# Turning the normed tiles of a fused two-layer attention kernel: on TensorE, or through memory and VectorE

## The chip, the core and the metric

The kernel runs on one core of a Trainium2 chip. A core has five engines that run their own instruction streams in order and wait for one another through semaphores: TensorE (PE; its weight loads are listed apart as PEld), VectorE (DVE), ScalarE (ACT), GpSimd (POOL) and SyncE (SP). DMAs are issued from the queues of SP, ScalarE and GpSimd and run on 16 DMA engines. A matmul writes to PSUM, from where VectorE or ScalarE fetch the result; tiles lie in SBUF, 128 partitions wide.

The metric is the time of one execution on the device in microseconds, as the median of several runs.

## What is computed

Two layers over an image batch `x` of 8 x 32 x 32 positions with 512 channels, all in float32. The first is a self-attention over the 1024 positions of an image (group norm, query, key and value products, softmax over 8 heads of 64, output product, residual). The second is a deformable attention:

```python
x_ln = layernorm(x, ln_g, ln_b)
q = x_flat @ wq + bq
o = gelu(depthwise_conv_7x7_stride_2(q_img, dw_w) + dw_b)     # 16 x 16 positions
offsets = conv_1x1(o, pw_w)                                   # 2 channels
grid = reference points + tanh(offsets)
interp = grid_sample(x, grid)                                 # 256 sampled rows
k = v = interp @ wv + bv
qh, kh, vh = heads(q @ mq_w + mq_b), heads(k @ mk_w + mk_b), heads(v @ mv_w + mv_b)
att = softmax(qh @ kh.T) @ vh
z = att @ mo_w + mo_b + x
out = gelu(layernorm(z, ln_g, ln_b) @ mlp_w + mlp_b) + z
```

The last three lines are where the change lies: `z` is normalised row by row (positions on partitions), and the product with `mlp_w` needs it with channels on partitions, so each normed tile of 128 positions x 512 channels has to be turned.

## The kernel before

**Two passes.** The first pass (L407 to L840) runs layer 0 for the eight images in 256 units and writes its output (`mid`) and the layer norm of it (`hat_d`) to memory; the depthwise convolution of the first six images is done beside it. The second pass (L843 to L1298) runs layer 1. Its unit is one pair of heads of one half image: 512 queries against 256 sampled keys. Eight units make an image (half images of four units each), 64 units make the pass.

**Order.** Every instruction keeps the order of the program on its engine (`InOrder`, L43). The program's order is written out by hand: `at(place, step)` puts a step at a place counted in units, and `run_due` emits the steps sorted by place. So a place says only what stands in front of what, on each of the five queues, not when it runs. A step at 7.012 stands behind all of those at 7.0 and ahead of those at 7.02, on every queue on which it has instructions.

**A unit n** (`unit_steps`, L1188). At n the scores (32 weight loads, `sc<-keys,q`), VectorE's row maxima (`nmax`) and ScalarE's exponentials (`e`). At n + 0.02 and n + 0.04 `moved` turns e in blocks of 32x32 on VectorE (`sq<-e`) and sends it to memory (`sq_d`, SP); at n + 0.0401 `taken` brings it back with keys on partitions (`et`, SP), in all a transpose through memory; `share` and `spread` do the same with the reciprocal sums (`rs_d`, `inv`, SP). At n + 0.042 stands the next unit's query product (`mm<-hat_h,wqq`). At n + 1.1 the product with the values (`av<-et,vals`), at n + 1.2 VectorE scales it (`attH`). So `av` of a unit runs at the end of the next one.

**The tiles of a half image** (`back_steps`, L1107). When four units have filled `attH`, the next four units each take one tile t of 128 positions, at n = start + t: `fetch` and `add` bring x's row (`xr`, SP) and add the bias to it (GpSimd); `joined` at n + 0.012 is the output product (`mm<-wo,attH`) and VectorE's z, its statistics, and the reciprocal root on GpSimd (`mv`); `norm` at n + 0.03 makes `zn` (VectorE). `turned` at n + 0.6 has four transposes on TensorE (`mm<-ident,zn`), whose result ScalarE copies to `zT`; `mlp` at n + 1.03 is the product with `wm`, in front of the next query product; `biased` (VectorE), `gelu` (ScalarE, for two tiles at n + 1.72 of the odd one), `end` (GpSimd, n + 2.24) finish it. Where the pass ends (`over`, `eve`, `tail`), other places hold.

**Beside the units.** The convolution of images 6 and 7 runs in two lanes (`conv_steps`, L1217): lane 0 has its taps on VectorE (5 per unit, 3 in the units in which the points are at work), lane 1 has 7 per unit, multiplied on ScalarE (`parts`) and added on GpSimd (`chunk`). The points of the next image (`point_steps`, L1242) come from convolution and offsets: some 20 tiny operations on VectorE (`targets`), an indirect DMA of four rows (`gather`, GpSimd) and the weighted sum (`sample`, VectorE) for each half of the points. Before the units, `prep` (L904) multiplies weights together and `load_late` (L1258) loads the rest, among it `wm`.

Of the kernel before, what the change touches and what calls it, by code (L numbers as in the profile page):

```python
# [247 lines left out]
def attention_then_deformable_attention(  # L248
# [119 lines left out]
    def at(place, step):  # L368
        due.append((place, len(due), step))
# [473 lines left out]
    with ExitStack() as l1:  # L843
# [23 lines left out]
        def load_small():  # L867
            with nc.allow_non_contiguous_dma(reason="small vectors onto partitions"):
                for t, v in (
                    (bvk, mk_b), (bv_c, bv), (bvv, mv_b), (bqq, mq_b), (bq_c, bq), (lng, ln_g),  # L870
                    (lnb, ln_b),
                ):
                    nc.sync.dma_start(t, v.rearrange("(c p) -> p c", p=P))

        def load_conv():
            with nc.allow_non_contiguous_dma(reason="small vectors onto partitions"):
# [68 lines left out]

        def conv_fetch(b, cb):
            chat[b, cb] = cvhat.tile([P, NT, P], F32, tag="hat", name="hat", bufs=2)
            nc.sync.dma_start(chat[b, cb], hat_d[b][:, :, ts(cb, P)])

        def conv_load(b):  # L950
            room[b, "o"] = cv.tile([P, NC, NS], F32, tag="o", name="o")
            nc.sync.dma_start(room[b, "o"], o_d[b][:, :, :])

        def fill(b, cb, par):
            hat = chat[b, cb]
# [117 lines left out]

        def fetch_hat(hi):
            hat[hi] = raw.tile([P, NC, C], F32, tag="hat", name="hat_h", bufs=2)
            nc.sync.dma_start(hat[hi], hat_d[hi // 2][:, ts(hi % 2, NC), :])

# [24 lines left out]
        def tmp(name, bufs):  # L1104
            return work.tile([P, C], F32, tag=name, name=name, bufs=bufs)

        def back_steps(hi, start, step, tail=False):  # L1107

            b, half = divmod(hi, 2)
            xs = mid[b].rearrange("(t p e) c -> e t p c", e=2, p=P)[half]  # L1110
            outs = out_tok[b].rearrange("(t p e) c -> e t p c", e=2, p=P)[half]
            xr, z, zn, zT, res = {}, {}, {}, {}, {}
            n_units = 2 * B * NHP

            def fetch(t):
                xr[t] = tmp("xr", 4)
                nc.sync.dma_start(xr[t], xs[t])

            def add(t):
                nc.gpsimd.tensor_tensor(xr[t], xr[t], bo_row, ALU.add)  # L1120

            def joined(t):
                ps = project(lambda c: attH[hi][:, c, ts(t, P)], lambda c: wo[:, c, :])
                z[t] = tmp("z", 4)
                nc.vector.tensor_tensor(z[t], ps, xr[t], ALU.add)
                stats = work.tile([P, 6], F32, tag="stats", name="stats")
                mv = xr["mv", t] = work.tile([P, 3], F32, tag="mv", name="mv")
                nc.vector.bn_stats(stats, z[t])
                nc.vector.bn_aggr(mv[:, 0:2], stats)
                rstd(mv[:, 2:3], mv[:, 1:2], 1e-5)  # L1130

            def norm(t):
                zn[t], mv = tmp("zn", 2), xr["mv", t]
                nc.vector.tensor_scalar(
                    zn[t], z[t], mv[:, 0:1], mv[:, 2:3], ALU.subtract, ALU.mult
                )

            def turned(t):
                ps = mm_tile()
                for c in range(NC):  # L1140
                    nc.tensor.transpose(ps[:, ts(c, P)], zn[t][:, ts(c, P)], ident)
                zT[t] = tmp("zT", 2)
                for half in range(2):
                    nc.scalar.copy(zT[t][:, ts(half, C // 2)], ps[:, ts(half, C // 2)])

            def mlp(t):
                res["ps", t] = project(lambda c: zT[t][:, ts(c, P)], lambda c: wm[:, c, :])

            def biased(t):
                res[t] = tmp("res", 3)  # L1150
                nc.vector.tensor_tensor(res[t], res["ps", t], bm_row, ALU.add)

            def gelu(t):
                nc.scalar.activation(res[t], res[t], AF.Gelu)

            def end(t):
                (nc.vector if tail else nc.gpsimd).tensor_tensor(res[t], res[t], z[t], ALU.add)
                (nc.sync if tail else nc.gpsimd).dma_start(outs[t], res[t])

            for t in range(NC):  # L1160
                over, eve = (start + step * t >= n_units - i and not tail for i in range(2))
                n, pair = start + step * t, start + step * (t - t % 2)

                ends = (n + 0.6, n + 1.03, n + 1.0392)
                if eve:
                    ends = (n + 0.61, n + 0.72, n + 0.73) if over else (n + 1.06, n + 1.62, n + 1.625)
                places = (pair - 1.6, pair - 0.5), (n + 0.012, n + 0.03), ends
                if tail:
                    turn = n + 0.15 + 0.005 * (t > 0)
                    places = (n - 0.7, n - 0.6), (n, n + 0.01), (turn, n + 0.25, n + 0.26)  # L1170
                steps = (fetch, add), (joined, norm), (turned, mlp, biased)
                for place, what in zip(sum(places, ()), sum(steps, ())):
                    at(place, lambda t=t, what=what: what(t))


                ends = [t - 1, t] if t % 2 and not tail else [t] if tail else []

                for what, after in (
                    (gelu, 0.27 if tail else 0.735 if over else 1.72),
                    (end, 0.28 if tail else 0.74 if over else 2.24),  # L1180
                ):
                    for i in ends:
                        at(n + after, lambda i=i, what=what: what(i))
# [33 lines left out]
        def conv_steps():  # L1217
            for lane, chunks in enumerate(((0, 3, 6), (1, 2, 4, 5, 7))):
                free = 0.5 + lane
                for k in chunks:  # L1220
                    b, cb = EARLY + k // NC, k % NC
                    first = next(n for n in range(60) if n + 0.49 > free)
                    fills = [first + 0.49, first + 0.55]
                    at(fills[0] - 1.8, lambda b=b, cb=cb: conv_fetch(b, cb))
                    for par, place in enumerate(fills):
                        at(place, lambda b=b, cb=cb, par=par: fill(b, cb, par))
                        at(place + 0.02, lambda lane=lane, par=par: fill_end(lane, par))
                    unit = int(fills[1]) + 1
                    i = 0
                    while i < KS * KS:  # L1230
                        points = unit % (2 * NHP) in (NHP - 1, NHP, NHP + 2)
                        count = 7 if lane else 3 if points else 5
                        for j in range(count):
                            if i == KS * KS:
                                break
                            place = 0.25 + 0.01 * j if not lane else 0.045 + 0.001 * j if j < 4 else 0.65 + 0.01 * j
                            at(unit + place, lambda b=b, cb=cb, i=i, lane=lane: tap(b, cb, i, lane))
                            free = unit + place
                            i += 1
                        unit += 1  # L1240

        def point_steps(b):  # L1242
            last = 2 * NHP * b - NHP
            at(last - 3.5, lambda: conv_load(b))
            at(last - 2.035, lambda: conv_gelu(b))
            at(last - 1.465, lambda: offsets(b))
            at(last - 1.36, lambda: offsets_turned(b))
            at(last - 0.959, lambda: targets(b))
            for h, (p0, p1) in enumerate(((-0.28, 0.0415), (1.72, 2.0415))):
                at(last + p0, lambda h=h: gather(b, h))  # L1250
                at(last + p1, lambda h=h: sample(b, h))
            first = 2 * NHP * b
            for hp, place in enumerate((-0.82, -0.815, 0.185, 1.18)):
                at(first + place, lambda hp=hp: key_step(b, hp))
            for t, place in enumerate((-0.81, 0.18)):
                at(first + place, lambda t=t: value_step(b, t))

        def load_late():  # L1258
            nonlocal bq_row, wo, wm, bo_row, bm_row
            bq_row = load_row(wp, bq, "bq_row")  # L1260
            wo = load_w(late2, mo_w, "wo")
            wm = load_w(late2, mlp_w, "wm")
            bo_row = load_row(late, mo_b, "bo_row")
            bm_row = load_row(late2, mlp_b, "bm_row")
            load_conv()
# [66 lines left out]
```

## Time and profile before

Three runs took 3374.16 to 3378.19 us, with a median of 3374.57. The profiled execution:

| what | value |
|---|---|
| time of the profiled execution | 3374.83 us |
| its span, from the first to the last instruction | 3373.1 us |
| mean granted TensorE clock | 0.991 |
| first scores of the second pass, about | 2217.7 us |
| zn transposes, `mm<-ident,zn` | 256, busy 41.8 us |
| copies of them, `zT<-mm`, ScalarE | 128, mean 373 ns |
| block transposes, `sq<-e`, 128x1024, VectorE | 640, mean 1228 ns |
| block transposes, `rsT<-rs`, 128x32, VectorE | 128, mean 212 ns |
| `nmax<-sc`, VectorE | 640, mean 1214 ns |
| lane 0 taps, `chunk<-pad,dww,chunk`, VectorE | 144, mean 760 ns |
| lane 1 adds, `chunk<-parts,chunk`, GpSimd | 240, mean 787 ns |
| `xr<-mid`, SP, 256 KB | 64, landing after 6.0 us (median) |

How to read it: the busy time of TensorE is the union of matmuls that overlap one another, so a busy TensorE is not one at its peak. A group's mean mixes places with different neighbours. In a timeline each row is a run of like instructions: start, time, engine, operation, output<-inputs, count, and in brackets how long the engine was idle before it and what ended that. A DMA's "us to landing" runs from its issue to the semaphore that tells that its data is there.

### The profile page before, as it was taken

The page shows a single profiled execution, that of the slowest core. Times are in us where ns is not written, and L with a number is a line of the kernel's source. Part 1 is how long each engine was busy: PE and PEld are TensorE (multiplying, and loading weights), DVE is VectorE, ACT ScalarE, POOL GpSimd, SP SyncE. Part 2 cuts the span into 40 slices and gives each one's busy share as a digit, 9 for nine tenths or more (in the row PEclk, how much of TensorE's full clock was granted, in tenths as well). Part 3 has the DMA queues.
Part 4 walks back from the last instruction along what each step waited for, and adds up shares of the span by engine and source line. Part 5 has one row for each costly group of instructions (what it writes and reads, how often), then busy time and mean ns, then how long its engine had stood idle before and what let it go on. Part 6 is the DMA issues. An engine that isn't in the chain of part 4 may idle for free. (4 is left out here: it accounts for less than half of the span.)

```text
span 3373.1 us, 59630 instructions
## 1 busy us (share of the span) xinstructions
PE 3282.7 (97%) x21736; PEld 1339.8 (40%) x21736; DVE 2490.4 (74%) x3373; ACT 1809.0 (54%) x3927; POOL 1548.1 (46%) x1903
## 2 busy tenths in 40 slices
PE   7999999999999999999999998889999999999998
PEld 3344444444444344344344443433333333333333
DVE  5777788888888898888888886238667686665654
ACT  3443355576566566567567562135556555654442
POOL 1001226646746755764765663305555454642222
PEclk9999999999999999999999999999999999999999
DMA  5666766776766776766777766546666665665653
GB/s 150 179 179 164 209 181 186 223 182 183 214 188 181 210 201 181 210 197 183 204 196 184 203 193 180 170 139 220 192 206 198 191 200 187 214 218 191 224 181 127
DMA packets 446645, 642.56 MB, mean 190 GB/s; under 512 B 77105, under 2 KB 240945, under 8 KB 444305
## 3 DMA queue, kind: packets, MB, share of 16 engines
q1 hardware_dynamic: 415712, 536.67, 55.0%
q0 software_dynamic: 29488, 100.00, 9.7%
q8 instruction: 172, 2.82, 0.4%
q10 hardware_dynamic: 1152, 2.10, 0.2%
q14 instruction: 121, 0.98, 0.1%
HBM read 246.38 MB, written 123.73 MB: 110 GB/s over the span
## 5 line engine op out<-in xcount | busy, mean ns | idle before, releaser
L54 ACT ACTIVATE e<-sc,nmax 128x1024 f32<-128x1024 f32 (+1 forms) x1024 | 802.0, 796 | 494.5 <-DVE nmax L54 493.1
L54 DVE TENSOR_REDUCE nmax<-sc 128x1 f32<-128x1024 f32 (+1 forms) x640 | 751.3, 1214 | 337.5 <-PE sc L54 336.8
L54 POOL TENSOR_TENSOR oa<-part_x,oa 128x256 f32<-128x256 f32 x852 | 639.6, 751 | 554.0 <-ACT part_x L54 507.6
L54 DVE STREAM_TRANSPOSE sq<-e 128x1024 f32<-128x1024 f32 x640 | 766.1, 1228 | 155.8 <-ACT e L54 134.6
L54 ACT ACTIVATE part_x<-pad_x,dww_x 128x256 f32<-128x256 f32 x852 | 440.9, 545 | 250.3 <-POOL oa L54 249.4
L54 PE MATMUL sc<-k,q 64*64 64x512 f32 x4096 | 516.6, 602 | 13.5 <-ACT e L54 10.3
L54 PE MATMUL av<-et,v 128*64 128x256 f32 x4096 | 502.1, 388 | 15.1 <-DMA et<-sq 14.2
L54 PE MATMUL mm<-xT,wqkv 128*64 128x512 f32 x2048 | 463.5, 595 | 3.2 <-issue 3.2
L54 PEld LDWEIGHTS av<-et,v 128*64 128x64 f32 x4096 | 275.5, 137 | 332.6 <-issue 169.8
L54 POOL TENSOR_TENSOR chunk<-parts,chunk 128x256 f32<-128x256 f32 x240 | 188.8, 787 | 268.5 <-ACT parts L54 254.5
L54 POOL TENSOR_TENSOR mv<-mv,minus_half 128x1 f32<-128x1 f32 x128 | 76.3, 596 | 510.4 <-DVE mv L54 509.8
L54 PEld LDWEIGHTS sc<-k,q 64*64 64x64 f32 x4096 | 139.3, 132 | 321.8 <-issue 205.0
L54 PEld LDWEIGHTS mm<-xT,wqkv 128*64 128x64 f32 x2048 | 148.6, 138 | 255.0 <-issue 239.6
L54 DVE SCALAR_TENSOR_TENSOR od<-pad_x,dww_x,od 128x256 f32<-128x256 f32 x276 | 232.0, 841 | 5.5
L54 PE MATMUL mm<-wo,attH 128*64 128x512 f32 x1024 | 233.7, 598 | 0.0
L54 PE MATMUL mm<-wqkv,xT 128*64 128x256 f32 x2048 | 232.1, 379 | 0.0
L54 PE MATMUL mm<-wm,zT 128*64 128x512 f32 x1024 | 230.7, 592 | 1.0 <-ACT zT L54 1.0
L54 PE MATMUL mm<-w,attT 128*64 128x512 f32 x1024 | 229.8, 592 | 1.8 <-DVE attT L54 1.8
L54 PE MATMUL mm<-hat_h,wqq 128*64 128x512 f32 x1024 | 230.8, 593 | 0.0
L54 ACT ACTIVATION_READ_ACCUMULATOR e<-sc,nmax 128x1 f32 x1024 | 209.3, 204 | 0.0
L54 ACT ACTIVATE parts<-pad,dww 128x256 f32<-128x256 f32 x240 | 126.4, 551 | 126.8 <-POOL chunk L54 125.9
L54 PEld LDWEIGHTS mm<-wqkv,xT 128*64 128x64 f32 x2048 | 147.9, 137 | 77.8 <-issue 6.4
(164 smaller groups left out, 3361.8 us busy)
## 6 DMA issues: line engine op xcount, KB each, us to landing
et<-sq SPq DMA_DIRECT2D x2048, 128.0 KB, 2.8
sq_d<-sq SPq DMA_DIRECT2D x128, 512.0 KB, 2.7
et<-sq_d SPq DMA_DIRECT2D x128, 512.0 KB, 4.5
inv<-rs_d SPq DMA_DIRECT2D x256, 128.0 KB, 5.3
hat_h<-hat_d SPq DMA_DIRECT2D x16, 1024.0 KB, 8.4
xr<-mid SPq DMA_DIRECT2D x64, 256.0 KB, 6.0
x<-in_x_dram POOLq DMA_DIRECT2D x60, 256.0 KB, 4.4
out_dram<-res POOLq DMA_DIRECT2D x60, 256.0 KB, 3.6
```

The lines of the kernel that those rows point to most:

```text
L54: return self.tc.keep_in_program_order(op(*args, **kwargs))
```

## The change

1. **Turning.** For 58 of the 64 tiles the four transposes on TensorE and ScalarE's two copies go. In their place: `away` writes zn to memory in four pieces (SP), `back` reads it (SP), with the blocks of 32 swapped between partitions and columns, and `blocks` transposes the 32x32 blocks on VectorE. The channels then lie on the partitions in another order, so `wm` is loaded in that order (four DMAs for one), and so are the vectors `lng` and `lnb` (eight small DMAs for two). The six tiles of the end (`by_matmul`) keep the transposes; `norm` writes them in the new order.
2. **The MLP's product** moves from n + 1.03 to n + 1.05, behind the next query product (n + 1.042) and in front of `av` (n + 1.1). `biased` moves from n + 1.0392 to n + 1.15, `end` from n + 2.24 to n + 2.0125.
3. **Points** are at work a unit sooner, but for the sampling, which stays; the gather moves from 0.72 to 0.0125 of the same unit. Lane 0 does 2 taps (3 before) in the units with sampling, and 5 in the unit that held the targets.
4. **Loads.** `xr` (a unit sooner as well, as is its bias), `hat_h` from the third half on, and the loads of `hat` and `o` go from SP's queue to ScalarE's.

```diff
         def conv_fetch(b, cb):
             chat[b, cb] = cvhat.tile([P, NT, P], F32, tag="hat", name="hat", bufs=2)
-            nc.sync.dma_start(chat[b, cb], hat_d[b][:, :, ts(cb, P)])
+            nc.scalar.dma_start(chat[b, cb], hat_d[b][:, :, ts(cb, P)])
...
-            nc.sync.dma_start(room[b, "o"], o_d[b][:, :, :])
+            (nc.scalar if b > 0 else nc.sync).dma_start(room[b, "o"], o_d[b][:, :, :])
...
-            nc.sync.dma_start(hat[hi], hat_d[hi // 2][:, ts(hi % 2, NC), :])
+            (nc.scalar if hi > 1 else nc.sync).dma_start(hat[hi], hat_d[hi // 2][:, ts(hi % 2, NC), :])
...
                 xr[t] = tmp("xr", 4)
-                nc.sync.dma_start(xr[t], xs[t])
+                nc.scalar.dma_start(xr[t], xs[t])
...
             def norm(t):
                 zn[t], mv = tmp("zn", 2), xr["mv", t]
+                to, src = zn[t], z[t]
+                if by_matmul(t):
+                    to = to.rearrange("p (c r i) -> p r c i", r=NSQ, c=NC)
+                    src = src.rearrange("p (r c i) -> p r c i", r=NSQ, c=NC)
                 nc.vector.tensor_scalar(
-                    zn[t], z[t], mv[:, 0:1], mv[:, 2:3], ALU.subtract, ALU.mult
+                    to, src, mv[:, 0:1], mv[:, 2:3], ALU.subtract, ALU.mult
+                )
+
+            def by_matmul(t):
+                return tail or start + step * t >= n_units - 1
+
+            def away(t):
+                zn["d", t] = dram.tile([NSQ, SQ, NSQ, P], F32, tag="zn_d", name="zn_d", bufs=3)
+                for k in range(NSQ):
+                    nc.sync.dma_start(
+                        zn["d", t][:, :, k].rearrange("r q x -> q r x"),
+                        zn[t][ts(k, SQ)].rearrange("q (r x) -> q r x", r=NSQ),
+                    )
+
+            def back(t):
+                zn["l", t] = tmp("zn", 2)
+                nc.sync.dma_start(zn["l", t], zn["d", t].rearrange("r q k x -> (r q) (k x)"))
+
+            def blocks(t):
+                zT[t] = tmp("zT", 2)
+                nc.vector.transpose(
+                    zT[t].rearrange("p (c k q) -> p k c q", c=NC, q=SQ),
+                    zn["l", t].rearrange("p (k c i) -> p k c i", k=NSQ, i=SQ),
                 )
...
-                ends = (n + 0.6, n + 1.03, n + 1.0392)
+                ends = (n + 0.0301, n + 0.0395, n + 1.013, n + 1.05, n + 1.15)
                 if eve:
                     ends = (n + 0.61, n + 0.72, n + 0.73) if over else (n + 1.06, n + 1.62, n + 1.625)
-                places = (pair - 1.6, pair - 0.5), (n + 0.012, n + 0.03), ends
+                places = (pair - 2.6, pair - 1.45), (n + 0.012, n + 0.03), ends
...
-                steps = (fetch, add), (joined, norm), (turned, mlp, biased)
+                turns = (turned,) if by_matmul(t) else (away, back, blocks)
+                steps = (fetch, add), (joined, norm), (*turns, mlp, biased)
...
-                    (end, 0.28 if tail else 0.74 if over else 2.24),
+                    (end, 0.28 if tail else 0.74 if over else 2.0125),
...
-                        points = unit % (2 * NHP) in (NHP - 1, NHP, NHP + 2)
-                        count = 7 if lane else 3 if points else 5
+                        points = unit % (2 * NHP) in (NHP, NHP + 2)
+                        count = 7 if lane else 2 if points else 5
...
-            at(last - 3.5, lambda: conv_load(b))
-            at(last - 2.035, lambda: conv_gelu(b))
-            at(last - 1.465, lambda: offsets(b))
-            at(last - 1.36, lambda: offsets_turned(b))
-            at(last - 0.959, lambda: targets(b))
-            for h, (p0, p1) in enumerate(((-0.28, 0.0415), (1.72, 2.0415))):
+            at(last - 4.5, lambda: conv_load(b))
+            at(last - 3.035, lambda: conv_gelu(b))
+            at(last - 2.465, lambda: offsets(b))
+            at(last - 2.36, lambda: offsets_turned(b))
+            at(last - 1.959, lambda: targets(b))
+            for h, (p0, p1) in enumerate(((-0.9875, 0.041), (1.0125, 2.041))):
                 at(last + p0, lambda h=h: gather(b, h))
                 at(last + p1, lambda h=h: sample(b, h))
...
-            wm = load_w(late2, mlp_w, "wm")
+            wm = late2.tile([P, NC, C], F32, tag="wm", name="wm")
+            for r in range(NSQ):
+                nc.sync.dma_start(
+                    wm[ts(r, SQ)], mlp_w.rearrange("(r c i) o -> r i c o", r=NSQ, c=NC)[r]
+                )
```

More of the change, by code (lines that the diff above doesn't have):

```diff
@@ L869, in load_small @@
                 for t, v in (
-                    (bvk, mk_b), (bv_c, bv), (bvv, mv_b), (bqq, mq_b), (bq_c, bq), (lng, ln_g),
-                    (lnb, ln_b),
+                    (bvk, mk_b), (bv_c, bv), (bvv, mv_b), (bqq, mq_b), (bq_c, bq),
                 ):
                     nc.sync.dma_start(t, v.rearrange("(c p) -> p c", p=P))
+                for t, v in ((lng, ln_g), (lnb, ln_b)):
+                    for r in range(NSQ):
+                        nc.sync.dma_start(
+                            t[ts(r, SQ)], v.rearrange("(r c i) -> r i c", r=NSQ, c=NC)[r]
+                        )
         def load_conv():
@@ L1261, in load_late @@
             wo = load_w(late2, mo_w, "wo")
-            wm = load_w(late2, mlp_w, "wm")
+            wm = late2.tile([P, NC, C], F32, tag="wm", name="wm")
+            for r in range(NSQ):
+                nc.sync.dma_start(
+                    wm[ts(r, SQ)], mlp_w.rearrange("(r c i) o -> r i c o", r=NSQ, c=NC)[r]
+                )
             bo_row = load_row(late, mo_b, "bo_row")
```

## The prediction

> **What bounds the kernel now.** I read the page's first part, then the busy time by stretch, then one unit of the second pass on TensorE and VectorE, then the DMA issues.
>
> ```profile
> span 3373.1 us, 59630 instructions
> PE 3282.7 (97%) x21736; PEld 1339.8 (40%) x21736; DVE 2490.4 (74%) x3373; ACT 1809.0 (54%) x3927; POOL 1548.1 (46%) x1903
> ```
>
> TensorE is busy for 97% of the span. Of seven stretches of whole units in the second pass (columns: PE, PEld, DVE, ACT, POOL, granted clock, DMA share, GB/s), four:
>
> ```profile
> 2634.00:2786.00 152.00, 147.34 (x906) 55.64 (x902) 106.07 (x169) 83.42 (x228) 76.58 (x90) 1.00 0.60 192
> 2786.00:2930.00 144.00, 140.85 (x878) 53.59 (x882) 98.54 (x161) 83.73 (x231) 76.32 (x90) 1.00 0.62 201
> 2930.00:3063.00 133.00, 133.00 (x842) 51.26 (x834) 81.90 (x134) 68.42 (x197) 50.09 (x58) 1.00 0.69 220
> 3063.00:3196.00 133.00, 133.00 (x842) 51.34 (x842) 82.17 (x134) 60.36 (x181) 37.15 (x40) 1.00 0.65 210
> ```
>
> From 2930 TensorE never stops: a microsecond taken off it there is a microsecond of the run. Earlier, while the convolution's taps still run beside the units, it stands idle 3 to 5 us in each stretch: from 2470 to 2930 the waits add up to 11.2 us (DVE res 5.0, zn 4.2, z 1.4, rs 0.6), and VectorE is the late one. One unit:
>
> ```profile
> 3128.27 1.89 PE L54 MATMUL av<-et,vals 128*64 128x512 f32 x8
> 3130.08 0.65 PE L54 MATMUL mm<-ident,zn 128*128 128x128 f32 x4
> 3130.67 1.96 PE L54 MATMUL sc<-keys,q 64*64 64x256 f32 x32
> 3132.56 3.65 PE L54 MATMUL mm<-wo,attH 128*64 128x512 f32 x16
> 3136.04 3.60 PE L54 MATMUL mm<-wm,zT 128*64 128x512 f32 x16
> 3139.47 3.60 PE L54 MATMUL mm<-hat_h,wqq 128*64 128x512 f32 x16
> 3142.91 1.89 PE L54 MATMUL av<-et,vals 128*64 128x512 f32 x8
> 3144.72 0.66 PE L54 MATMUL mm<-ident,zn 128*128 128x128 f32 x4
> ```
>
> The period is 3144.72 - 3130.08 = 14.64 us, and from the transposes' first load to the scores' is 3130.67 - 3130.08 = 0.59. VectorE in a tap unit (its scores began at 2594.94, from the weight loads):
>
> ```profile
> 2596.44 0.65 DVE L54 TENSOR_TENSOR attH<-av,inv 128x512 f32<-128x512 f32 x1
> 2597.01 3.96 DVE L54 SCALAR_TENSOR_TENSOR chunk<-pad,dww,chunk 128x256 f32<-128x256 f32 x5
> 2600.90 2.34 DVE L54 TENSOR_REDUCE nmax<-sc 128x4 f32<-128x1024 f32 x2
> 2603.17 0.68 DVE L54 TENSOR_TENSOR z<-mm,xr 128x512 f32<-128x512 f32 x1
> ...
> 2604.82 0.15 DVE L54 TENSOR_SCALAR mv<-mv 128x1 f32<-128x1 f32 x1
> ...
> 2615.40 5.55 DVE L54 SCALAR_TENSOR_TENSOR chunk<-pad,dww,chunk 128x256 f32<-128x256 f32 x3
> ```
>
> From attH to mv's end is 8.5 us without a gap: in the changed order the transposed zT comes right behind this mv.
>
> **What is taken off TensorE.** Of 64 tiles six keep the transposes (two of the last half but one, four of the tail), so 58 lose them. Before: av's last loads, a pause of 0.52 us (the weight loads' gap in front of the transposes is 0.81, elsewhere 0.29), then 0.59. I leave the pause in: in the first pass the output product takes 3.74 from first load to next first load where scores follow it, and 3.22 where another product of its own tile shape does. So 58 x 0.59 = **34.2 us** come off (64 if the pause went too), and the clean unit becomes 14.05. ScalarE loses 2 x 0.373 per tile, for which TensorE waited 1.0 us in all.
>
> **What is put on VectorE.** One block transpose of 128x512: rows 128x32 at 0.212 and 128x1024 at 1.228 give 0.212 + 480 x (1.016 / 992) = 0.70; bounds 0.61 (half the large one) and 1.23. The MLP's product now stands behind the query's, at 1.89 + 3.06 + 3.43 = 8.38 us into the unit. Clean unit: z starts at 5.59 to 5.66, 1.75 later comes the transpose, 0.70 more: 8.0 to 8.1. It is in time by 0.3 us; at 1.23 it would be 0.2 late, 22 times, 5 us.
> Tap units: five taps stand behind attH, which starts some 0.1 after the scores. 0.1 + 8.5 + 0.1 + 0.7 = 9.4, so the MLP's product waits **1.05 us** where five taps precede a unit without extra products (units 4 and 6 of eight). Sampled units (5 and 7 of eight): POOL now has gather (4 x 1.28) and both xr adds (2.5) in units 3 and 5, with seven chunk adds of 0.8 and the power: 13.8 of 14 us. ScalarE's last taps and both GELUs wait on it, so e in units 4 and 6 starts about 10 us in. For unit 4, of 15.1 us by then: first e 11.9, its sq 13.1, zn, sums and second sq 15.2, sampling 18.3, res 18.9, attH 19.4, which is 4.3 in unit 5; two taps 5.9, nmax 8.1, z to mv 10.0, zT 10.6, less 8.38: 2.2 us of waiting. Unit 7, behind the same chain half a microsecond later: 2.7. Units 7, 0, 1 and 2 carry keys, values and fills, in which VectorE catches up. Lane 0 taps run until unit 37. Counted: units 6 and 7 3.75, 12 and 13 3.25, 20 to 23 7.0, 28 to 31 7.0, 36 to 39 4.25: **25 us** of new waits. Bounds: 5 (the moved POOL adds no longer hold up taps: 0.59 each where POOL is still, against 0.77) and 45 (taps as the last row above shows them, 1.85 each, while POOL adds wide tiles).
> These lie in the same units as the 11.2 us of old waits, which they replace: xr's add comes a unit earlier, and zn has no reader on TensorE.
>
> [...]
>
> **What is put on SP's queue.** Four writes and one read per tile. An issue: sq_d's 0.32, inv's 0.62 for more pieces; I take 0.42, 1.7 for four. The read waits for all writes and the second sq_d, both et and both inv stand behind it.
>
> ```profile
> sq_d<-sq SPq DMA_DIRECT2D x128, 512.0 KB, 2.7
> et<-sq_d SPq DMA_DIRECT2D x128, 512.0 KB, 4.5
> inv<-rs_d SPq DMA_DIRECT2D x256, 128.0 KB, 5.3
> ```
>
> Clean unit: zn at 9.8, writes issued by 11.5, landed at 14 (2.4 to 2.7, as rs_d and sq_d; bounds 2.0 and xr's 6.0), read, then sq_d at 14.4 instead of 11.7. The second et is issued at 17.6 instead of 15.1 and lands at 22 to 23.5; av is due at 25.9 (was 26.45, et at 20 to 21.5). Hidden by 2.4 us or more; without that cover each microsecond costs one per unit. zn comes back some 17 us after the scores, and its transpose is due at 21. In return xr (64 x 0.52), hat_h (14) and the loads of o and hat leave SP for ScalarE's queue: about 0.5 us per tile there, ahead of taps 5 to 7, GELU and the next e, against 0.75 taken away: nothing.
>
> **The rest, each near nothing.** Six more small loads (0.51) end before SP's wait at 2131.73 plus 2.4, and their product comes at 2149.2. Three more pieces of wm put o's load back by 1.1 to 2.6 us; it landed at 2166.3 and was read at 2174.0. Six tiles normed into another order: 0.51, up to 1.49 beside POOL, so -0 to +4 in the tail. Units 0 to 5: the points' chain moves from unit 3 to 2 and lane 0 does two more taps; VectorE's work there is the same, ±4.
>
> **Sum.** 3373.1 - 34.2 - 11.2 + 25 = 3352.7 of span; the profiled execution took 3374.83, 1.7 more, and the median is 3374.57: **3354 us**.
>
> **Rivals.**
> - *VectorE keeps up.* Points a unit sooner and fewer taps beside sampling leave 5 us of waits: 3374.8 - 45.4 + 5 = 3334. For it: POOL's wide adds leave the stretch of the taps. Against: the 8.5 us row.
> - *Off TensorE, onto VectorE.* Waits reach 45: 3374, no change. For it: 106 of 152 us busy, in order, plus 0.7 per tile. Against: VectorE then is as slow as in the worst unit, everywhere.
> - *SP's queue is late: slower.* If four writes land in 6.6 us, not 2.5 (hat_d from rows did, and xr took 6.0), the second sq_d, et and inv are 4 us later still, and av waits about 1.3 us in each of 58 units: 3354 + 75 less what VectorE's waits share with it (25) = 3404. It decides above some 5 us of landing. For it: 512 B pieces and a DMA share of 0.6 to 0.7 already. Against: 2.4 to 2.9 for sq_d, rs_d, mid.
>
> **How the numbers follow.** Forecast (3343 to 3366) 0.48; VectorE keeps up 0.22; no change 0.12; SP late 0.18. Faster by over 0.2% (6.7 us, about what a measurement here can tell) is the first two, 0.70; within it 0.12; slower 0.18. The range takes in the 5 and 45 us ends with ±4 of start and tail, and the lower edge of the third rival: 3330 to 3386.
>
> **What would show it.** Right: no zn transposes but 24, a clean unit of 14.05, mm<-wm,zT waiting on DVE zT in units 4 to 7 of eight before unit 40 alone. Rival one: hardly any such waits. Rival three: av waiting on et, SP waiting on zn_d. Wrong altogether: ScalarE's e late in clean units, from DMA issues waiting ahead of it.

## The result, and the profile after

The changed kernel takes 3407.44 us (median of four runs, 3403.39 to 3412.38) against 3376.38 for the kernel before beside it: a ratio of 1.0089, with a 95% interval of 1.0066 to 1.0111. It is slower by some 30 us, where the forecast had it 20 us faster. The profiled execution took 3412.38 us.

The page's head and chain of the changed kernel:

```profile
span 3410.6 us, 59716 instructions
PE 3280.1 (96%) x21504; PEld 1333.4 (39%) x21504; DVE 2514.1 (74%) x3431; ACT 1794.0 (53%) x3823; POOL 1551.5 (45%) x1903
...
PE 22%; DMA 6%; DVE 3%; issue 2%; POOL 1%; ACT 1%; SPq 1%; another core or an unknown queue 0%; POOLq 0%; ACTq 0%; DVEq 0%
PE mm L54 17%; DMA et<-sq_d 3%; PE av L54 2%; PE sc L54 2%; DMA sq_d<-sq 1%; DMA zn_d<-zn 1%; POOL chunk L54 1%; SPq L54 1%; DVE nmax L54 1%; DVE chunk L54 0%; ACT e L54 0%; POOL row L54 0%; DVE sq L54 0%; DMA inv<-rs_d 0%; DVE zn L54 0%
```

The chain by engine of the kernel before, for comparison:

```profile
PE 27%; ACT 3%; DVE 2%; POOL 2%; DMA 1%; issue 1%; SPq 0%; ACTq 0%; POOLq 0%; DVEq 0%
```

TensorE is busy for only 2.6 us less than before, though 232 of its matmuls are gone. DMAs hold 6% of the chain, 1% before, and half of that is et<-sq_d, the read that brings the turned exponentials back. Two stretches of the second pass, by the starts of the scores' weight loads units 8 to 40 and 40 to 63 (columns: PE, PEld, DVE, ACT, POOL, granted clock, DMA share, GB/s):

```profile
2349.00:2949.00 600.00, 569.44 (x3436) 213.91 (x3432) 434.76 (x703) 329.25 (x860) 307.58 (x359) 0.99 0.73 222
2949.00:3341.00 392.00, 376.43 (x2285) 141.38 (x2284) 226.62 (x381) 173.38 (x488) 114.42 (x127) 0.98 0.70 223
```

The second stretch is the one in which TensorE never stopped before. Now it stands still for 392.00 - 376.43 = 15.6 us there, at a clock of 0.98 instead of 1.00. What it waits for, in the whole run (us in total, times, longest):

```profile
PE mm L54 <- DVE zT L54: 27.1, 17, 3.2
PE av L54 <- DMA et<-sq_d: 25.9, 13, 6.8
```

Before there was no first line, and the second had 3.5 us in two waits. From 2949 to 3341 zT has 0.2 us and et 14.5 us in five waits. What SP's queue waits for, from 2310 to 3310, in the changed kernel:

```profile
SPq L54 <- DVE sq L54: 272.5, 55, 13.1
SPq L54 <- DMA sq_d<-sq: 159.9, 54, 4.8
SPq L54 <- DMA zn_d<-zn: 132.3, 84, 5.3
SPq L54 <- DMA et<-sq_d: 27.0, 14, 6.1
```

And in the kernel before:

```profile
SPq L54 <- DVE sq L54: 561.2, 108, 17.0
SPq L54 <- DMA sq_d<-sq: 64.4, 50, 2.9
```

The first line is SP's idle time, in which it waits for new work. Half of it is gone. One round of SP in a clean unit (a unit without taps of the convolution or extra products beside it), from one first sq_d to the next:

```profile
3043.80 0.34 SPq L54 DMA_DIRECT2D sq_d<-sq  x1
3044.23 3.95 SPq L54 DMA_DIRECT2D zn_d<-zn  x4
3048.28 0.40 SPq L54 DMA_DIRECT2D rs_d<-rsT  x1
3053.37 0.34 SPq L54 DMA_DIRECT2D zn<-zn_d  x1
3053.80 0.38 SPq L54 DMA_DIRECT2D sq_d<-sq  x1
3054.28 3.96 SPq L54 DMA_DIRECT2D et<-sq_d  x2
3058.30 1.24 SPq L54 DMA_DIRECT2D inv<-rs_d  x2
3059.58 1.37 SPq L54 DMA_DIRECT2D sq_d<-sq  x1
```

After rs_d nothing is issued for 4.7 us: the read stands in front, and SP waits 4.6 us there for zn_d, until the writes have landed. The second sq_d, both et and both inv stand behind it. The round takes 3059.58 - 3043.80 = 15.8 us, of which only 0.7 us are waits for an engine, and TensorE's unit takes 14.05. So SP falls back by up to 1.7 us in such a unit, until av has to wait:

```profile
3060.96 1.02 PE L54 MATMUL av<-et,vals 128*64 128x512 f32 x2
3068.73 3.62 PE L54 MATMUL av<-et,vals 128*64 128x512 f32 x6 [6.75 <-DMA et<-sq_d]
3072.28 1.96 PE L54 MATMUL sc<-keys,q 64*64 64x256 f32 x32
```

Six matmuls of av took 3.62 us there, when eight take 1.89: TensorE came back from the pause at a lower clock (0.50 granted from 3070 to 3072).

The falling back can be followed over several units. In the four from 3145.75 on, the read is issued at 3148.22, 3165.64, 3181.56 and 3197.32, the last two rounds 15.9 and 15.8 us long, while the units take 14.8; it stands 2.5, 3.3, 4.4 and 5.4 us into its unit, and in the fourth av waits 3.05 us. Not every round is that long: in the four units from 3283.88 on, the read stands 2.8, 0.8, 3.1 and 0.9 us into its unit, and av does not wait. In the units with keys and values, which take some 16 to 22 us, SP catches up.

### The profile page after: what moved, and what is told of

The parts are those of the page before. It is cut to its first block, busy times and chain, and to the rows that moved or that the text cites. A ratio compares the mean times of both kernels' runs of the same rounds, so it can differ in the third digit from the quotient of the medians.

```text
span 3410.6 us, 59716 instructions
## 1 busy us (share of the span) xinstructions
PE 3280.1 (96%) x21504; PEld 1333.4 (39%) x21504; DVE 2514.1 (74%) x3431; ACT 1794.0 (53%) x3823; POOL 1551.5 (45%) x1903
## 3 DMA queue, kind: packets, MB, share of 16 engines
q14 instruction: 124, 1.02, 0.1%
## 5 line engine op out<-in xcount | busy, mean ns | idle before, releaser
L54 PE MATMUL mm<-wm,zT 128*64 128x512 f32 x1024 | 236.7, 605 | 28.1 <-DVE zT L54 27.1
```

The lines of the kernel that those rows point to most:

```text
L54: return self.tc.keep_in_program_order(op(*args, **kwargs))
```

## The experiments

Three theories stood at the start. T1: the order on SP's queue; the read waits for a landing, and what stands behind it is late. T2: the load; the trip's bytes slow every transfer, wherever they stand. T3: the rest of the change (loads on ScalarE's queue, points sooner, order of the products). Beside them the late zT in the tap units, which the forecast had. Times in the table are medians, ratios go to the kernel before on the same chip; the stretches (from the starts of the scores) and waits are from the profiled execution of each, which is the slowest run of the changed kernel and of e4_memory_from_40 and the fastest of e5 and e6, some 5 to 10 us from the median. The kernel before has medians of 3373.5 to 3376.4 us on the chips used, so medians of different rows compare to within some 3 us.

| kernel | us | ratio (95%) | units 8-40 | 40-63 | av waits for et | mm for zT |
|---|---|---|---|---|---|---|
| before | 3376.38 | | 587.7 | 376.1 | 3.5 | |
| changed | 3407.44 | 1.0089 (1.0066-1.0111) | 599.4 | 392.3 | 25.9 | 27.1 |
| e1_read_behind | 3485.81 | 1.0313 (1.0287-1.0340) | 637.4 | 417.7 | 8.7 | 107.1 |
| e2_all_tensore | 3381.51 | 1.0011 (0.9997-1.0025) | 590.7 | 376.1 | 8.0 | |
| e3_unit_later | 3344.80 | 0.9908 (0.9882-0.9934) | 563.4 | 364.3 | 12.1 | 0 |
| e4_memory_from_40 | 3396.85 | 1.0048 (1.0033-1.0064) | 590.7 | 397.1 | 24.7 | 2.7 |
| e5_later_read_ahead | 3374.49 | 1.0003 (0.9991-1.0015) | 569.4 | 381.8 | 31.4 | 0 |
| e6_trip_unread | 3415.93 | 1.0127 (1.0110-1.0144) | 601.9 | 393.0 | 27.2 | |
| e7_trip_unread_behind | 3377.97 | 1.0011 (1.0002-1.0021) | 593.0 | 376.1 | 4.5 | |
| e8_memory_until_40 | 3390.44 | 1.0052 (1.0035-1.0069) | 600.5 | 376.1 | 15.7 | 25.5 |
| e9_later_end_mended | 3341.65 | 0.9897 (0.9880-0.9913) | 563.7 | 364.3 | 10.8 | 0 |

**The read behind (e1_read_behind).**

```diff
-                ends = (n + 0.0301, n + 0.0395, n + 1.013, n + 1.05, n + 1.15)
+                ends = (n + 0.0301, n + 0.0412, n + 1.013, n + 1.05, n + 1.15)
```

> The changed kernel, with one step moved: the read of the turned tile is issued on SP behind the scores, et and inv of its unit, not ahead of them. The same DMAs, the same bytes. T1 (order on SP: sq_d and et stand behind a read that waits some 5 us for four writes to land): av's waits for et fall from 25.9 us to under 8; the read lands 1 to 1.5 us later than zT's place in a clean unit allows, so that zT's waits rise from 27 to 30 to 55; 3375 to 3392. T2 (the added traffic slows every transfer, whatever stands first): av's waits stay at 20 us or more, 3400 to 3412. T3 (the cost lies in the moved loads and the points): av's waits stay, 3400 to 3412.

av's waits fell to 8.7 us, close to what T1 has (under 8), but the waits for zT rose to 107.1 us (30 to 55 expected) and the time missed every expectation: 3485.81. The read landed far later than the 1 to 1.5 us that I had allowed, and not only TensorE stood behind it. VectorE, then TensorE, of this kernel:

```profile
3055.60 0.15 DVE L54 TENSOR_SCALAR mv<-mv 128x1 f32<-128x1 f32 x1
3062.23 0.71 DVE L54 STREAM_TRANSPOSE zT<-zn 128x512 f32<-128x512 f32 x1 [6.47 <-DMA zn<-zn_d]
3062.86 1.20 DVE L54 STREAM_TRANSPOSE sq<-e 128x1024 f32<-128x1024 f32 x1
```

```profile
3053.64 3.60 PE L54 MATMUL mm<-hat_h,wqq 128*64 128x512 f32 x16
3063.09 6.33 PE L54 MATMUL mm<-wm,zT 128*64 128x512 f32 x16 [5.84 <-DVE zT L54]
3069.24 1.90 PE L54 MATMUL av<-et,vals 128*64 128x512 f32 x8
```

The block transpose waits on VectorE for its data, and the sq transposes of the unit wait behind it, so sq_d, et and the next read are late too: the delay feeds itself. And the MLP's product takes 6.33 us instead of 3.60 after its pause. This run alone does not settle T1 against T2, since the wait only changed its place.

**All tiles on TensorE (e2_all_tensore).**

```diff
             def by_matmul(t):
-                return tail or start + step * t >= n_units - 1
+                return True
...
-                ends = (n + 0.0301, n + 0.0395, n + 1.013, n + 1.05, n + 1.15)
+                ends = (n + 0.6, n + 1.05, n + 1.15)
```

> The changed kernel with all 64 tiles turned on TensorE, in the transposes' old place, and nothing through memory; the MLP product behind the query's, the points a unit sooner and the loads on ScalarE's queue stay. T1 and T2 (both lay the cost on the trip through memory): av's waits for et back under 5 us, no waits for zT; 3360 to 3378, at or a little under the kernel before. T3 (the moved loads and points cost the time): 3395 to 3410, with no gain from taking the trip out.

3381.51, 3.5 us above the range of T1 and T2 and not to be told from the kernel before (the interval holds 1); av's waits, 8.0 us, are also above the 5 expected. T3 falls: the loads on ScalarE's queue, the points and the order of the products cost at most 0.25%, and 40 to 63 takes 376.1 us as before.

**Everything behind the writes a unit later (e3_unit_later).** The core of the edit; the two units ahead of the tail keep TensorE's transposes (57 tiles go through memory, not 58), the MLP's product stands in front of the next query product again, and gelu and end follow.

```diff
-                return tail or start + step * t >= n_units - 1
+                return tail or start + step * t >= n_units - 2
...
-                ends = (n + 0.0301, n + 0.0395, n + 1.013, n + 1.05, n + 1.15)
+                ends = (n + 0.0301, n + 0.0412, n + 1.0405, n + 2.03, n + 2.0392)
```

> The changed kernel with everything behind the writes a unit later: the read behind inv, VectorE's transpose in the next unit behind attH, the MLP product after the output product of the unit behind that, gelu and end a unit later too; the tiles of the last two units before the tail on TensorE. T1: av's waits for et under 8 us and zT's waits under 5, since the read has a whole unit to land; the 34 us of the removed transposes are then kept for the most part: 3338 to 3362. T2: zT's waits go but av's stay at 15 us or more: 3380 to 3400.

3344.80, in T1's range: faster than the kernel before by 0.7 to 1.2%. av's waits of 12.1 us are above T1's 8, but only 0.9 us of them lie in units 8 to 63. Its two stretches (columns as above):

```profile
2342.00:2905.00 563.00, 560.31 (x3432) 208.13 (x3424) 434.58 (x706) 319.15 (x852) 310.38 (x359) 1.00 0.76 236
2905.00:3269.00 364.00, 363.07 (x2288) 135.44 (x2287) 226.39 (x382) 163.82 (x480) 110.69 (x123) 1.00 0.76 242
```

TensorE does the same matmuls as in the changed kernel, but stands still 3.6 us instead of 46.1, at full clock, while the DMA share is higher (0.76 against 0.70 to 0.73). A round of its SP queue in a clean unit:

```profile
3108.71 0.34 SPq L54 DMA_DIRECT2D sq_d<-sq  x1
3109.14 2.91 SPq L54 DMA_DIRECT2D zn_d<-zn  x4
3112.15 0.40 SPq L54 DMA_DIRECT2D rs_d<-rsT  x1
3112.67 1.23 SPq L54 DMA_DIRECT2D sq_d<-sq  x1
3114.25 3.92 SPq L54 DMA_DIRECT2D et<-sq_d  x2
3118.26 1.28 SPq L54 DMA_DIRECT2D inv<-rs_d  x2
3119.59 0.63 SPq L54 DMA_DIRECT2D zn<-zn_d  x1
3122.84 0.34 SPq L54 DMA_DIRECT2D sq_d<-sq  x1
```

The same twelve issues; the gap in front of the read is gone, because the writes land while the others are issued (from 2310 to 3310 SP waits 0.7 us for zn_d, 132.3 in the changed kernel). The queue is through at 3120.22, 11.5 us after the first sq_d, and has 2.6 us left until the next.

**The trip only from unit 40, and only until 39 (e4_memory_from_40, e8_memory_until_40).** The first edit; the second has `>= 40` in its place.

```diff
-                return tail or start + step * t >= n_units - 1
+                return tail or start + step * t >= n_units - 1 or start + step * t < 40
```

> The changed kernel with the trip through memory only from unit 40 on (no taps of the convolution beside it there); the tiles of units 0 to 39 turned on TensorE. T1 and T2: units 8 to 40 take 580 to 590 us (599.4 in the changed kernel), units 40 to 63 stay at 388 to 394 us (376.1 before), since there SP is late whatever VectorE does; 3384 to 3398. If instead the late zT of the tap units is what makes SP late further on, units 40 to 63 fall to 365 or less and the time to 3360 or less.

> The changed kernel with the trip through memory only up to unit 39, TensorE's transposes from unit 40 on. It gives the price of the tap units by themselves: units 8 to 40 at 595 to 602 us (599.4 in the changed kernel, 590.7 with all tiles on TensorE), units 40 to 63 at 375 to 378; 3383 to 3394 in all. If the late et of the clean units had come from the tap units' delay, 40 to 63 would stay above 385 and the time at 3400.

Both times came in their ranges, and e8's stretches too; e4's two stretches, 590.7 and 397.1 us, lie above theirs. Alone from unit 40, the trip costs 397.1 - 376.1 = 21.0 us there, with no late zT in front of it, though 23 x 0.59 = 13.6 should have come off. Alone until 39 it costs 600.5 - 590.7 = 9.8 where 32 x 0.59 = 18.9 should have come off, and 40 to 63 is untouched. The two losses are separate.

**The read ahead, its consumer a unit later (e5_later_read_ahead).** As e3_unit_later, with the read's place 0.0395 again.

```diff
-                ends = (n + 0.0301, n + 0.0412, n + 1.0405, n + 2.03, n + 2.0392)
+                ends = (n + 0.0301, n + 0.0395, n + 1.0405, n + 2.03, n + 2.0392)
```

> The kernel in which everything behind the writes comes a unit later (the one measured at 3345), with one step put back: the read is issued on SP ahead of the scores, et and inv, as in the changed kernel. With it and the three others the place of the read and the place of its consumer stand in all four combinations. [...] Rival (the read's place cost nothing; what the later consumer mended was zT alone): av's waits stay under 15, 3342 to 3350.

3374.49: one place on SP's queue is worth 30 us. av's waits rise by 19.3 us to 31.4, and the rival (under 15 us, 3342 to 3350) falls; T1 had 25 us or more here, with 3360 to 3390 as the author's estimate, and both came. The time rises by 1.5 times the added waits. A lower clock explains little of that: in units 8 to 63 of this kernel the granted clock lies below 1.00 by only 1.7 us in sum. There TensorE stands still 17.0 us instead of 3.6 in e3_unit_later, and av's matmuls are busy 117.8 us instead of 107.6, which may be short waits inside their runs; that is not shown. SP waits 119.9 us for zn_d again (0.7 with the read behind):

```profile
SPq L54 <- DMA sq_d<-sq: 205.8, 59, 5.7
SPq L54 <- DMA zn_d<-zn: 119.9, 92, 6.1
```

**The trip alone, used by nothing (e6_trip_unread, e7_trip_unread_behind).** On top of e2_all_tensore; the second has 0.0412.

```diff
+                if not (tail or start + step * t >= n_units - 1):
+                    at(n + 0.0301, lambda t=t: away(t))
+                    at(n + 0.0395, lambda t=t: back(t))
```

> All tiles turned on TensorE as in the kernel measured at 3382, and besides the four writes and the read at the changed kernel's places; what is read back is used by nothing, so this is the trip's price on SP and the DMA engines alone. T1: the read ahead of et makes av wait 15 to 30 us in units 40 to 63 as well as before, 3395 to 3415. Rival (SP has slack enough while the unit still takes 14.64 us; only the shorter unit makes it late): 3380 to 3388.

> The same unused trip with the read behind the scores, et and inv on SP. T1 (order): av's waits for et under 10 us, 3378 to 3390. T2 (the added traffic and issues themselves): the same time as with the read ahead, 3395 or more.

With the read ahead 3415.93, a microsecond above T1's range, and 393.0 us from 40 to 63; with the read behind 3377.97 and 376.1. That is what the kernel without any trip takes: each is 1.0011 of the kernel before on its chip. The bytes and the issues are the same in both. T2 falls: the traffic costs nothing that shows. The rival in e6 falls too: SP is late even where the unit still takes 14.64 us.

By the place of the read and of its consumer (medians; without a trip it is 3381.51):

| | consumer in the same unit | a unit later | nobody |
|---|---|---|---|
| read ahead of sq_d, et, inv | 3407 | 3374 | 3416 |
| read behind them | 3486 | 3345 | 3378 |

**The end mended (e9_later_end_mended).** As e3_unit_later; for the tile of unit 62:

```diff
-                    ends = (n + 0.6, n + 1.03, n + 1.0392)
+                    ends = (n + 0.6, n + 1.05, n + 1.15)
```

> The kernel in which everything behind the writes comes a unit later, with its last unit mended: there two MLP products came together, the second one's bias add stood on VectorE between the two transposes of sq, and the second et came 3 us later than in the kernel before. The second product and its bias add go behind av, and behind sq. If the end is what that order costs, the stretch from the last unit's scores to the end falls from 74.0 us to 68 to 71 and the time to 3338 to 3343; if et is late there for the load alone, it stays at 73 to 75 and 3344 to 3348.

3341.65. From the last unit's scores to the end it is 3341.0 - 3269.7 = 71.3 us, a little above the range, 74.0 in e3_unit_later; the intervals of the two ratios overlap, so the gain is likely but not shown. It is the best median of all, 0.9 to 1.2% below the kernel before.

## Why the prediction was wrong, step by step

- **Off TensorE, 34.2 us: right.** A clean unit of the changed kernel in which nothing waits goes from scores at 3131.70 to scores at 3145.75, the 14.05 forecast. In e3_unit_later the 55 units from 8 to 63 take 927.6 us against 966.8 with the transposes, 39.2 less: TensorE's busy time falls by 30.0 (55 x 0.59 = 32.5 were forecast), and it stands still 9.2 us less.
- **On VectorE: right as a wait, short as a cost.** The block transpose takes 0.70 us, and a clean zT ends 8.1 us into its unit (3153.15 + 0.70 - 3145.75), as forecast. The waits for zT were put at 25 us in units 6 to 39 and are 24.2 there, all in units 4 to 7 of eight, as forecast (27.1 in the whole run; the 2.9 behind unit 40 were not forecast). That the sum is so near is in part chance: unit 4 of eight was put at 1.05 us and has 2.1, unit 5 at 2.2 and has 0.3 to 1.6. (The sum's 9.4 - 8.38 is 1.02, not 1.05, and the 0.59 us of a tap with POOL still is that of the five of 2629.13, where GpSimd was still only from 2630.24 on; the five of 2540.86, beside which it did nothing, took 0.51 each. Neither matters here.) What was left out is that TensorE can be slow after a pause (5.35 us for a product that else takes 3.60, below).
- **The old waits vanish: right.** No wait of TensorE for res or zn is left in the waits of the changed kernel.
- **SP's queue, "Hidden by 2.4 us or more": the step that failed.** It followed one unit from a queue that stood idle: writes issued by 11.5 us, landed at 14, second et issued at 17.6. Two of its terms were too small. The issues of the four writes were put at 1.7 us and take 3.1 on average over the 58 tiles (1.8 to 9.0; in the longest, 6.1 us are a wait of SP for the landing of et<-sq_d). From the last of them to the read it is 3.3 us on average (1.4 to 5.9), against 2.5 for the landing. Above all the step did not add up the queue's whole round. That is 15.8 us in the round shown against 14.05, so the delay is not a fixed amount per unit, but grows until something gives way, and then TensorE stands for up to 6.8 us at once. The margin to check was the queue's time per period, not one transfer's distance to its reader.
- **The rest, nothing: right** as far as it can be told (e2_all_tensore, 0.9997 to 1.0025, is -1 to +8 us).
- **A term that was missing.** From 8 to 63 the changed kernel takes 24.8 us more than e2_all_tensore (991.6 against 966.8). TensorE stands still 46.1 us instead of 12.8, 33.3 more, and its busy time, which should have fallen by 32.5, fell by 954.0 - 945.5 = 8.5. So 24 us went into matmuls that were busy for longer. They lie in the two groups that wait: av's 440 matmuls (103.7 to 121.8, 18.0 us) and the MLP's product (198.1 to 204.0, 5.8); scores, query and output products are within 1 us. Of the 5.8, three runs of 5.35 us behind pauses of 2.11, 2.14 and 3.24 us make 5.1. The granted clock lies below 1.00 by 11.8 us in sum over these stretches (in windows of 8 us, pauses among them), which explains at most half of the 24; whether short waits for pieces of et inside av's runs make up the rest is not shown. How av's 18 us divide stays open.

In sum the step "SP" cost 29.8 us against the forecast in units 40 to 63 (16.2 more than before instead of 13.6 less) and the tap units, 8 to 40, missed by 20.3 (11.7 more instead of 8.6 less); there TensorE's busy time fell by 7.8 us instead of 18.9, and av waited 5.4 us for et beside the waits for zT. The rest of the profiled execution's excess is 7.2 us in the first pass (its first scores come at 2224.9, against 2217.7 before and 2217.2 in e6, which has the same loads, so a scatter of runs is likely) and 2 us in the tail. The third rival named the mechanism, its signs (av waiting for et, SP waiting for zn_d) and, at 3404, nearly the time. It had it by another road, though: 1.3 us in each of 58 units, which would need a landing of 6.6 us. The waits are in fact few and long, and the mean of 3.3 us behind the writes is nearer to the forecast's 2.5 than to that, so its nearness to the measured time is in part chance. The evidence against it, "2.4 to 2.9 for sq_d, rs_d, mid", was true of the kernel before and did not bear on the queue's round.

## What to carry to other kernels

When a step that waits for a landing is put on a queue in order, add up that queue's whole round, issues and waits, and compare it with the period of the engine that bounds the kernel; slack seen for one transfer does not show that the round fits. Put the waiting step behind everything that is ready, and its consumer a whole period later: here nearly the same instructions (57 or 58 tiles through memory) took 3486, 3407, 3374 or 3345 us by these two places. An order that hides a trip for one engine may hold another: a transpose that waited on VectorE (6.47 us in the rows of e1_read_behind) held the work that would have fed the next unit.

## What the runs showed of the hardware

**TensorE came back slow from six of nine pauses of over 2 us.** Rows of the changed kernel, two of them behind pauses of the same length, then its granted clock around the pause before av (column after POOL's busy time):

```profile
2427.80 3.60 PE L54 MATMUL mm<-hat_h,wqq 128*64 128x512 f32 x16
2433.52 5.35 PE L54 MATMUL mm<-wm,zT 128*64 128x512 f32 x16 [2.11 <-DVE zT L54]
2438.67 1.92 PE L54 MATMUL av<-et,vals 128*64 128x512 f32 x8
...
2738.66 3.65 PE L54 MATMUL mm<-wm,zT 128*64 128x512 f32 x16 [2.11 <-DVE zT L54]
```

```profile
3068.00:3073.00 5.00, 4.27 (x22) 1.29 (x26) 0.61 (x1) 0.00 (x0) 0.00 (x0) 0.58 0.18 44
3073.00:3077.00 4.00, 4.00 (x38) 1.65 (x32) 2.43 (x3) 1.40 (x7) 0.00 (x0) 1.00 0.92 288
```

The pause of 2.11 us before 2433.52 cost another 1.7 in the product behind it, at a granted clock of 0.57 from 2433.5 to 2436; the one of 2.11 us before 2738.66 cost nothing, at 1.00. Of the nine pauses of over 2 us in units 8 to 63, six were followed by a lower clock (0.50 from 3070 to 3072, 0.52 to 0.61 in the 2.5 to 2.9 us behind the others) and three (2.11, 2.13 and 2.35 us) were not (1.00). In e1_read_behind even one of 3.05 us (before 2766.56) cost nothing. There, where the MLP's product waited 92.8 us in units 8 to 63, its busy time grew from 198.2 to 235.4: 0.4 us for each microsecond of waiting. What decides which pause is followed by a lower clock is not shown.

**Added traffic cost nothing by itself.** A trip of 256 KB out and back per unit, read by nobody, left the time where it was (1.0011 of the kernel before, as without it) with the read behind the other issues on SP. Nor did the landings differ much: sq_d took 3.3 us to land (median) and et 5.3 in e3_unit_later, with 57 trips, against 3.2 and 5.3 in e2_all_tensore, without any (2.7 and 4.5 in the kernel before).

**SP stood in front of the read until the writes had landed.** From 2310 to 3310 it waited 119.9 us for zn_d in e5_later_read_ahead and 124.5 in e6_trip_unread, with the read ahead, and 0.7 and 0.8 in e3_unit_later and e7_trip_unread_behind, with the read behind. The price of standing there was 30 to 38 us by what stands behind (3374.49 - 3344.80 and 3415.93 - 3377.97).
